# A four-layer graph network on one core: edge scores turned onto feature partitions, and five kept row blocks in the attention layer

## The chip, the cores and the metric

The kernel runs on one core of one Trainium2 chip. The metric is the device time of one execution in microseconds; less is better. Before the change three runs took 4965.81, 4971.25 and 4976.65 us, the median is 4971.25 us.

The engines are named as the profile names them: PE is the matrix engine (PEld its weight loads), DVE the vector engine, ACT the scalar engine, POOL the engine that issues gathers and scatters, SP the one that issues plain DMAs. SBUF is the working memory, PSUM the memory that matmuls write.

## The reference

There are 6250 nodes with 256 features, and 100,000 edges src -> dst, sorted by dst. Four layers follow each other, each ending in a layer norm of x plus the layer's output: a linear layer summed over edges, a two-matrix network on gathered sums, another with weighted edges and batch norms, and an attention layer. What the change touches is the attention layer's score of an edge and its sum:

```
h = lrelu(x @ w_W + w_b)                              # slope 0.2
edge_h = lrelu(edge_attr @ ew_W + ew_b)               # 100000 x 128 by 128 x 256
e = concat(h[src], h[dst], edge_h) @ a_W + a_b        # a_W is 768 x 1
alpha = exp(e - max over the edges of src)  /  their sum over the edges of src
out = sum over the edges of src of alpha * h[dst]
```

The third part of e, edge_h @ a_W[512:768], depends on the inputs only. This "edge score" is computed at the kernel's start, and used at its end.

## The kernel before, in words

The work starts with `prepare` (from L1909). Edges are split into 782 columns of up to 128 edges. Each edge becomes a record of four numbers (target node, place of its source in its block, edge weight, edge score), and the records have to be sorted by source block. For that DVE and PE count edges per block and rank them (`Slots`), and each column's 128 records are scattered to a table in DRAM by one indirect DMA on POOL (`Scatter.columns`, L929). The first 192 columns ("own", PLACED) are not scattered: they are put in place by matmuls with one-hot matrices (`Placed`: `build` makes the matrices on DVE, L880 to L897; `use` multiplies, L909).

The edge scores (`Scores`, L749 to L850) go through the columns in chunks of twelve (STEP), loaded by one DMA each (L802), and in units of four columns. The order of chunks is written out: seven scattered chunks, then sixteen groups of one own chunk and two scattered ones (nine units), then the scattered rest, twelve chunks of which two have one column. There are some 197 units. `turn` transposes a unit's four columns on PE (L813), and ACT copies them out (L815). `score` then makes, for each column, a PSUM tile with the edges on partitions and the 256 features along it: a matmul of three bf16 rows with ones brings the bias (L824), a matmul adds the column's features times the weight in fp32 (L825). A 257th column of the weight holds the part of the score that is linear. DVE reads the tile, takes the maximum with 0, multiplies by 0.8 a and sums (L827), and ACT adds the 257th column and writes the record's score (L829). Then the column may be scattered.

`run` (L833) puts other work between the units: unit i is turned, unit i - 1 scored, an own unit built after two and used after three, and a table of extras adds the second part of the ranks in units 2 to 18 (L728 to L731), the transposes and the first linear layer of 49 node blocks from unit 33 on, three units apart (L357, L364, L1997, L940, L941), and counts of edges by target block from unit 41 on (49 times L2031). This order is a wish: outside of stretches marked manual_schedule the framework's scheduler orders the instructions of each engine itself, as long as data and buffers allow it. Inside such stretches (the attention layer is one) they stand as written. A pool's buffers are handed out in turn, so the next user of a buffer waits for the last one.

When the last record is scattered, `read_lists` (L1677) reads the table back, and the other layers run. The attention layer is `direct_l3` (L1475). It goes through 49 source blocks of 128 nodes; each has 17 tiles of 128 edges (S_TILES), sorted by target block. Tiles whose targets all lie below block H3 are "near": their rows are kept in SBUF (`hot`) and reached by matrices; every other tile's rows are gathered by an indirect DMA (L979). `near_tiles` (L1048) counts the near ones: three of 17 for nearly all blocks. The stages of several blocks are interleaved by a table of steps (L1659):

- `rows` (lag 0) gathers the far tiles; `scores` (lag 1) adds the gathered half of the score (L1539) and spreads scores over partitions by transposes (L1550), four tiles to one PSUM tile.
- `matrices` (lag 2) makes, for each kept block, a matrix from one-hots (L1621: three bf16 parts for each pair of near tile and block), ACT copies it (L1624).
- `largest` takes the maximum (L1560), and asks for the transposes of tiles 12 to 16 after its first step; `parts` and `weights` make the exponents (L1569 to L1603); ACT makes three scaled one-hots for a near tile (L1601) and one for a far tile (L1603).
- `sums` (lag 2) adds far rows (L1630) and kept rows (L1633), fp32, two passes each; `means` and `finish` (lag 3) end the block.
- `masks` (L1514 to L1518) and `near_scores` (L1529, L1532: the kept half of the score for near tiles) prepare the next block on DVE.

Of the kernel before, what the change touches and what calls it, by code (L numbers as in the profile page):

```python
# [7 lines left out]
FT = mybir.dt.float32  # L8
I32 = mybir.dt.int32
AF = mybir.ActivationFunctionType  # L10
OP = mybir.AluOpType
# [39 lines left out]
S_TILES = sum(n for _, _, _, n in STRETCHES)  # L51
TS = NB * S_TILES
S_ROWS = -(-(S_TILES * P * NB + E) // P)
H0, H1, H2, H3 = 24, 16, 9, 3
SURE = 3.5


# [691 lines left out]
class Scores:  # L749
# [4 lines left out]

    STEP = 12

    def __init__(self, k, pool, psum, attr, ew_w, ew_b, a_w, out, ready):
        self.k, self.pool, self.psum, self.attr, self.out, self.ready = k, pool, psum, attr, out, ready
        nc, v = k.nc, k.nc.vector
        self.w = pool.tile([P, D + 1], FT, name="ew_w")  # L760
        nc.sync.dma_start(self.w[:, :D], ew_w)
        self.a = bcast_row(k, pool, a_w[2 * D:3 * D, :], D, "a3")
        self.b = pool.tile([3, D + 1], BF16, name="ew_b8")
        with k.tc.tile_pool(name="score_in", bufs=1) as tmp:
            b = tmp.tile([P, D + 1], FT, name="ew_b")
            nc.sync.dma_start(b[:, :D], bass.AP(tensor=ew_b.tensor, offset=ew_b.offset, ap=[[0, P], [1, D]]))
            for t in (self.w, b):
                scr = tmp.tile([P, D], FT, name="a_scr")
                v.scalar_tensor_tensor(scr, t[:, :D], SLOPE, self.a, op0=OP.mult, op1=OP.mult,
                                       accum_out=t[:, D:D + 1])  # L770
            v.tensor_scalar(self.a, self.a, 1.0 - SLOPE, None, op0=OP.mult)

            here = tmp.tile([3, 3], FT, name="ew_here")
            v.tensor_scalar(here, k.iota_row[:3, :3], k.iota_p[:3, :], None, op0=OP.is_equal)
            part = tmp.tile([3, D + 1], BF16, name="ew_part")
            v.memset(self.b, 0.0)
            for i in range(3):
                v.tensor_copy(part, b[:3, :])
                if i < 2:
                    v.tensor_sub(b[:3, :], b[:3, :], part)  # L780
                v.scalar_tensor_tensor(self.b, part, here[:, i:i + 1], self.b, op0=OP.mult, op1=OP.add)
        self.ones = pool.tile([3, P], BF16, name="ones3")
        nc.gpsimd.memset(self.ones, 1.0)

        own, other = list(range(0, PLACED, self.STEP)), list(range(PLACED, EC, self.STEP)) + [EC]
        self.order = other[:7]
        for i, c in enumerate(other[7:]):
            if i % 2 == 0:
                self.order += own[i // 2:i // 2 + 1]
            self.order.append(c)  # L790
        assert len(self.order) == len(own) + len(other)
        self.units = [(c, min(4, EC - c), P) for c0 in self.order if c0 < EC
                      for c in range(c0, min(c0 + self.STEP, EC), 4)] + [(EC, 1, ET)]
        self.at, self.a_t = {}, {}

    def load(self, c):
        if c % self.STEP and c != EC or c > EC or c in self.at:
            return
        at = self.at[c] = self.pool.tile([P, self.STEP, DE], FT, name="at", bufs=2)
        if c < EC:  # L800
            n = min(self.STEP, EC - c)
            self.k.nc.sync.dma_start(at[:, :n, :],  # L802
                                     self.attr[c * P:(c + n) * P, :].rearrange("(c p) d -> p c d", p=P))
        else:
            self.k.nc.sync.dma_start(at[:ET, 0, :], self.attr[P * EC:E, :])

    def turn(self, pool, i):
        c0, n, n_e = self.units[i]
        at, off = (self.at[EC], 0) if c0 == EC else (self.at[c0 // self.STEP * self.STEP], c0 % self.STEP)
        w_all = (n - 1) * P + n_e  # L810
        pa = self.psum.tile([P, 4 * P], FT, name="ps_a")
        for j in range(n):
            self.k.nc.tensor.transpose(pa[:, j * P:j * P + n_e], at[:n_e, off + j, :], self.k.ident[:n_e, :n_e])  # L813
        a_t = self.a_t[i] = pool.tile([P, 4 * P], FT, name="a_t", bufs=3)
        self.k.nc.scalar.copy(a_t[:, :w_all], pa[:, :w_all])  # L815

    def score(self, pool, i):
        nc = self.k.nc
        c0, n, n_e = self.units[i]
        a_t = self.a_t.pop(i)  # L820
        s = pool.tile([P, 4], FT, name="half", bufs=4)
        for j in range(n):
            z = self.psum.tile([P, D + 1], FT, name="ps_b", bufs=3)
            nc.tensor.matmul(z[:n_e, :], self.ones[:, :n_e], self.b, start=True, stop=False)  # L824
            nc.tensor.matmul(z[:n_e, :], a_t[:, j * P:j * P + n_e], self.w, start=False, stop=True)  # L825
            scr = pool.tile([P, D], BF16, name="scr", bufs=2)
            nc.vector.scalar_tensor_tensor(scr[:n_e, :], z[:n_e, :D], 0.0, self.a[:n_e, :], op0=OP.max, op1=OP.mult,  # L827
                                           accum_out=s[:n_e, j:j + 1])
            nc.scalar.activation(self.out[:n_e, c0 + j:c0 + j + 1], z[:n_e, D:], AF.Identity, bias=s[:n_e, j:j + 1])  # L829
        if c0 >= PLACED:  # L830
            self.ready(c0, c0 + n)

    def run(self, pool, extra):  # L833

        n = len(self.units)
        for i in range(n + 3):
            if i < n:
                c0 = self.units[i][0]
                if c0 in self.order:
                    for c in self.order[self.order.index(c0):][:2]:  # L840
                        self.load(c)
                self.turn(pool, i)
            if 0 <= i - 1 < n:
                self.score(pool, i - 1)
            for lag, f in ((2, "build"), (3, "use")):
                if 0 <= i - lag < n and self.units[i - lag][0] < PLACED:
                    getattr(self.placed, f)(self.units[i - lag][0])
            for f in extra.get(i, ()):
                f()
        assert not any(i > n + 2 for i in extra)  # L850


class Placed:
# [29 lines left out]
    def build(self, c0):  # L883
# [8 lines left out]
        slot = []  # L892
        for j in range(4):
            lo, hi = IN[c0 + j]
            slot.append(self.pool.tile([P, max(h - l for l, h in IN) * P], F32R, name="placed_l", bufs=8))
            nc.vector.tensor_scalar(slot[-1][:, :(hi - lo) * P], k.iota16[:, :(hi - lo) * P],
                                    self.at[:, c0 + j:c0 + j + 1], None, op0=OP.is_equal)  # L897
        self.rhs[c0] = rhs, slot
# [1010 lines left out]
def prepare(k, a, table0, first, rec, placed, ends, idx_d, loc_d, bad):  # L1909
# [6 lines left out]
    with (  # L1916
# [44 lines left out]
        with tc.tile_pool(name="score", bufs=1) as pool:  # L1961
# [29 lines left out]
                transposed(k, x_ts[b], load_block(k, pool, a["x"], b))  # L1991

            def row(b):
                ph = ps.tile([P, D + 1], FT, name="ps_b", bufs=3)[:, :D]
                times(k, ph, x_ts.pop(b), w_t)
                h = pool.tile([P, D], FT, name="h", bufs=2)
                nc.vector.tensor_add(h, bias, ph)  # L1997
# [85 lines left out]
            at(40, blocks)  # L2083
            for b in range(NB):
                at(41 + b // 2, count, b)
            scores.placed = None
            scores.run(pool, extra)


# [50 lines left out]
```

## Time and profile before

| | |
|---|---|
| median of the runs | 4971.25 us |
| the profiled execution | 4276.06 us |
| its span | 4274.2 us |
| mean granted PE clock | 0.925 |
| PE busy | 3609.2 us (84%) |
| DVE busy | 2950.7 us (69%) |
| POOL busy | 2738.1 us (64%) |
| ACT busy | 1476.9 us (35%) |
| L825 with 1564 passes on PE | 548.5 us |
| L929, 590 scatters on POOL | 578.7 us |
| L979 on x, 541, and on rows, 1032 gathers | 557.5 and 1154.2 us |

The profiled execution is one run, and was shorter than the three timed ones. Its page has no row that says why. Busy time is the time in which an engine works on an instruction; for PE the ends are modelled, so that the distance between starts says more than durations. A wait line reads: who waited, for whom, us in total, times, longest. "Issue" is time in which the profile shows nothing that was waited for.

The stages by time: the scores with their scatter 70 to 986 us, layer one to about 1580, layer two to about 2330, layer three to about 3240, the attention layer to the end.

### The profile page before, as it was taken

The numbers are of one execution on the slowest core, as the hardware profiler recorded it, in microseconds if no ns is written. First come the engines' busy times: TensorE is split into PE (matmuls) and PEld (weight loads), VectorE is DVE, ScalarE is ACT, GpSimd is POOL, SyncE is SP. The second block draws the span as 40 slices with busy tenths as digits, with TensorE's granted clock in tenths as the row PEclk, the third lists the DMA queues.
The fourth block names the chain that finished last, engine by engine and source line by source line (L and its number), as shares of the span: only waits on it lengthen the run. The fifth ranks groups of instructions, "written<-read, shape, count | busy, mean of one in ns | idle before, by whom it ended". The sixth has DMA issues, their size and how long they took to land. (4 is left out here: it accounts for less than half of the span.)

```text
span 4274.2 us, 70822 instructions
## 1 busy us (share of the span) xinstructions
PE 3609.2 (84%) x23988; PEld 2791.3 (65%) x23988; DVE 2950.7 (69%) x9234; ACT 1476.9 (35%) x3780; POOL 2738.1 (64%) x2685
## 2 busy tenths in 40 slices
PE   7999999985999988888886999999853777777776
PEld 4566666644999977766665777777532565656565
DVE  7887665544777757878787665565286777777775
ACT  1344334332333322222222111111343455555554
POOL 3765656576777757566663777777303777777774
PEclk9999999997999989989998999999997888888888
DMA  4233333325766775455563333333244444444443
GB/s 82 61 89 91 92 87 84 88 54 140 217 215 210 218 229 166 135 167 173 169 186 92 110 108 107 108 109 108 58 113 126 124 134 142 134 140 136 137 137 91
DMA packets 373432, 552.44 MB, mean 129 GB/s; under 512 B 88710, under 2 KB 265064, under 8 KB 372774
## 3 DMA queue, kind: packets, MB, share of 16 engines
q0 software_dynamic: 136064, 353.87, 29.2%
q1 hardware_dynamic: 236998, 193.96, 15.2%
q8 instruction: 193, 3.16, 0.3%
q14 instruction: 177, 1.45, 0.1%
HBM read 486.32 MB, written 62.09 MB: 128 GB/s over the span
## 5 line engine op out<-in xcount | busy, mean ns | idle before, releaser
L979 POOL DMA_INDIRECT g<-rows,idx_s x1032 | 1154.2, 1118 | 388.2 <-issue 239.0
L929 POOL DMA_INDIRECT rec<-r_s,addr x590 | 578.7, 981 | 337.5 <-ACT r_s L829 227.1
L979 POOL DMA_INDIRECT g<-x,idx_s x541 | 557.5, 1030 | 220.7 <-issue 77.1
L979 POOL DMA_INDIRECT g<-rows,idx_d x383 | 434.7, 1135 | 269.5 <-PE ps_g L986 157.4
L825 PE MATMUL ps_b<-ew_w,a_t 128*128 128x257 f32 x1564 | 548.5, 433 | 2.0 <-ACT a_t L815 2.0
L827 DVE SCALAR_TENSOR_TENSOR scr<-ps_b,a 128x256 bf16<-128x256 f32 x782 | 325.1, 423 | 254.3 <-PE ps_b L825 229.8
L1630 PE MATMUL ps_g<-g,s 128*128 128x257 f32 x1374 | 406.3, 466 | 0.0
L1130 PEld LDWEIGHTS <-od 128*128 128x128 bf16 x5947 | 348.7, 98 | 53.4 <-issue 20.4
L1630 PEld LDWEIGHTS ps_g<-g,s 128*128 128x128 f32 x1374 | 324.2, 240 | 63.5
L1138 PE MATMUL ps_g<-g,cs 128*128 128x256 f32 x1082 | 290.1, 395 | 44.7 <-DMA g<-x,idx_s 43.3
L829 ACT ACTIVATE r_s<-ps_b,half 128x1 f32<-128x1 f32 x782 | 201.1, 263 | 360.5 <-DVE scr L827 355.3
L974 DVE TENSOR_TENSOR os<-iota_row,loc_s 128x768 bf16<-128x768 f32 (+3 forms) x294 | 271.2, 922 | 72.9 <-PE ps_q L1284 62.2
L1092 DVE TENSOR_SCALAR od<-iota,rel 128x128 bf16<-128x128 f16 (+9 forms) x780 | 248.8, 399 | 100.6 <-PE ps_q L1130 96.4
L825 PEld LDWEIGHTS ps_b<-ew_w,a_t 128*128 128x128 f32 x1564 | 233.5, 188 | 97.1 <-ACT a_t L815 2.3
L1133 ACT CAST a_hi<-ps_q 128x512 fp32r<-128x512 f32 x294 | 172.6, 587 | 328.9 <-PE ps_q L1130 321.9
L1550 PE MATMUL ps_a<-ident,ep 128*128 128x128 f32 x833 | 154.8, 315 | 148.5 <-DVE ep L1539 100.1
L1133 ACT COPY a_hi<-ps_q 128x512 f32<-128x512 f32 x146 | 70.0, 480 | 590.2 <-PE ps_q L1130 570.5
L985 PE MATMUL ps_g<-g,cs 128*128 128x256 f32 x728 | 234.1, 338 | 43.0 <-DMA g<-rows,idx_d 41.9
L1138 PEld LDWEIGHTS ps_g<-g,cs 128*128 128x128 f32 x1082 | 186.3, 190 | 106.5 <-DMA g<-x,idx_s 85.4
L1287 ACT CAST a_hi<-ps_q 128x512 fp32r<-128x512 f32 x196 | 114.9, 586 | 381.8 <-PE ps_q L1284 368.3
L985 PE MATMUL ps_g<-first_rows,a_hi 128*128 128x256 f32 x980 | 245.6, 283 | 0.0
L986 PE MATMUL ps_g<-first_rows,a_hi 128*128 128x256 f32 x980 | 244.4, 282 | 0.0
(294 smaller groups left out, 8195.1 us busy)
## 6 DMA issues: line engine op xcount, KB each, us to landing
at<-in_edge_attr SPq DMA_DIRECT2D x65, 768.0 KB
edge_row<-node_row SPq DMA_DIRECT2D x49, 544.0 KB
xb<-x SPq DMA_DIRECT2D x144, 128.0 KB
g<-rows,idx_s POOLq DMA_INDIRECT x1032
xb<-in_x SPq DMA_DIRECT2D x96, 128.0 KB
x<-x SPq DMA_DIRECT2D x96, 128.0 KB
rows<-hl SPq DMA_DIRECT2D x47, 256.0 KB
rec<-r_s,addr POOLq DMA_INDIRECT x590
```

The source lines that it names most:

```text
L825: nc.tensor.matmul(z[:n_e, :], a_t[:, j * P:j * P + n_e], self.w, start=False, stop=True)
L827: nc.vector.scalar_tensor_tensor(scr[:n_e, :], z[:n_e, :D], 0.0, self.a[:n_e, :], op0=OP.max, op1=OP.mult, accum_out=s[:n_e, j:j + 1])
L929: s = nc.gpsimd.indirect_dma_start(out=self.table, out_offset=bass.IndirectOffsetOnAxis(ap=self.addr[:n, c:c + 1], axis=0), in_=self.rec[: ...
L974: k.nc.vector.tensor_tensor(dst, k.iota_row.unsqueeze(1).to_broadcast([P, n, P]), loc.unsqueeze(2).to_broadcast([P, n, P]), op=op)
L979: k.nc.gpsimd.indirect_dma_start(out=dst, out_offset=None, in_=table, in_offset=bass.IndirectOffsetOnAxis(ap=idx, axis=0))
L985: k.nc.tensor.matmul(out, lhs, row[:, :D].bitcast(F32R), start=start, stop=False)
L986: k.nc.tensor.matmul(out, lhs, row[:, D:2 * D].bitcast(F32R), start=False, stop=stop)
L1092: nc.vector.tensor_scalar(od[:, o:o + (hi - lo) * P], k.iota16[:, :(hi - lo) * P], rel[:, s + t:s + t + 1], None, op0=OP.is_equal)
L1130: nc.tensor.matmul(pa[:, j * P:(j + 1) * P], od[:, o:o + P], x[:, t, :], start=(m == 0), stop=(m == len(steps) - 1))
L1133: nc.scalar.copy(a[:, :n, :].rearrange("p j s -> p (j s)"), pa[:, :n * P])
L1138: nc.tensor.matmul(ps, a, row, start=start, stop=stop)
L1630: nc.tensor.matmul(ps, s[:, j, :], g[:, j, :D + 1], start=(j == 0), stop=False)
```

## The change

In the scores the features go onto partitions, and the edges of a unit, 512, along the tile. With a the score's weight and W, b those of the edge features, each output feature's column of W is scaled by |a| (so the product with the edge is |a| p). As |a| lrelu(p + b) = 0.2 |a| b + max(|a| p + 0.8 |a| b, 0.2 |a| p), ACT adds the shift 0.8 |a| b while it copies the product out of PSUM, and DVE takes the maximum of that and of 0.2 times the product, which it reads from PSUM too. The two feature halves are joined by one DVE instruction with the product of their signs, and a matmul with the sign vector, one for each column of edges, sums over partitions. Twelve columns' sums stand in one PSUM tile, to which ACT adds the constant 0.2 a b and writes the records; only then are the twelve scattered, or built and used if they are own. The bias matmuls, the 257th column, and the accumulating DVE instructions go. The PSUM tiles called ps_b become two of 512 columns instead of three of 257 (the node blocks' linear layer uses them too), ps_t is new; a_t has two buffers instead of three, the own columns' one-hots (placed_l) six instead of eight. `sums` runs two units after `hidden`.

In the attention layer H3 goes from three to five. Then four of 17 tiles are near (three in the last block, with 14 gathers left), 13 are gathered; the pairs of near tile and kept block go from six to ten, and the matrices of five blocks take two PSUM tiles instead of one.

```diff
-H0, H1, H2, H3 = 24, 16, 9, 3
+H0, H1, H2, H3 = 24, 16, 9, 5
...
-    def score(self, pool, i):
+    def hidden(self, pool, i):
+        nc = self.k.nc
+        w = self.units[i][1] * P
+        a_t = self.a_t.pop(i)
+        y = pool.tile([P, DK, 4 * P], FT, name="y", bufs=2)
+        for o in range(DK):
+            pz = self.psum.tile([P, 4 * P], FT, name="ps_b", bufs=2)
+            nc.tensor.matmul(pz[:, :w], self.w[:, 0, o * P:(o + 1) * P], a_t[:, :w], start=True, stop=True)
+            z = pool.tile([P, 4 * P], FT, name="z", bufs=3)
+            nc.scalar.activation(z[:, :w], pz[:, :w], AF.Identity, bias=self.shift[:, o:o + 1])
+            nc.vector.scalar_tensor_tensor(y[:, o, :w], pz[:, :w], SLOPE, z[:, :w], op0=OP.mult, op1=OP.max)
+        v = self.v[i] = pool.tile([P, 4 * P], FT, name="v", bufs=3)
+        nc.vector.scalar_tensor_tensor(v[:, :w], y[:, 0, :w], self.signs, y[:, 1, :w], op0=OP.mult, op1=OP.add)
+
+    def sums(self, pool, i):
         nc = self.k.nc
         c0, n, n_e = self.units[i]
-        a_t = self.a_t.pop(i)
-        s = pool.tile([P, 4], FT, name="half", bufs=4)
+        first = self.of(c0)
+        if c0 == first:
+            self.rows[first] = self.psum.tile([P, self.STEP], FT, name="ps_t", bufs=1)
+        pt, v = self.rows[first], self.v.pop(i)
         for j in range(n):
-            z = self.psum.tile([P, D + 1], FT, name="ps_b", bufs=3)
-            nc.tensor.matmul(z[:n_e, :], self.ones[:, :n_e], self.b, start=True, stop=False)
-            nc.tensor.matmul(z[:n_e, :], a_t[:, j * P:j * P + n_e], self.w, start=False, stop=True)
-            scr = pool.tile([P, D], BF16, name="scr", bufs=2)
-            nc.vector.scalar_tensor_tensor(scr[:n_e, :], z[:n_e, :D], 0.0, self.a[:n_e, :], op0=OP.max, op1=OP.mult,
-                                           accum_out=s[:n_e, j:j + 1])
-            nc.scalar.activation(self.out[:n_e, c0 + j:c0 + j + 1], z[:n_e, D:], AF.Identity, bias=s[:n_e, j:j + 1])
-        if c0 >= PLACED:
-            self.ready(c0, c0 + n)
+            c = c0 - first + j
+            nc.tensor.matmul(pt[:, c:c + 1], v[:, j * P:(j + 1) * P], self.sign[:, 1:2], start=True, stop=True)
+        end = c0 + n
+        if end - first == self.STEP or end == EC or c0 == EC:
+            nc.scalar.activation(self.out[:n_e, first:end], pt[:n_e, :end - first], AF.Identity, bias=self.same[:n_e, :])
+            self.ready(first, end)
...
             if 0 <= i - 1 < n:
-                self.score(pool, i - 1)
-            for lag, f in ((2, "build"), (3, "use")):
-                if 0 <= i - lag < n and self.units[i - lag][0] < PLACED:
-                    getattr(self.placed, f)(self.units[i - lag][0])
+                self.hidden(pool, i - 1)
+            if 0 <= i - 3 < n:
+                self.sums(pool, i - 3)
+            if self.todo:
+                for f, c in self.todo.pop(0):
+                    f(c)
...
+    def ready(self, c0, c1):
+        if c0 >= PLACED:
+            self.scatter(c0, c1)
+        else:
+            p, c = self.placed, range(c0, c1, 4)
+            for i in range(len(c) + 1):
+                self.todo.append([(p.use, x) for x in c[max(i - 1, 0):i]] + [(p.build, x) for x in c[i:i + 1]])
...
-            slot.append(self.pool.tile([P, max(h - l for l, h in IN) * P], F32R, name="placed_l", bufs=8))
+            slot.append(self.pool.tile([P, max(h - l for l, h in IN) * P], F32R, name="placed_l", bufs=6))
...
-                ph = ps.tile([P, D + 1], FT, name="ps_b", bufs=3)[:, :D]
+                ph = ps.tile([P, D], FT, name="ps_b", bufs=2)
```

In the steps ahead, "L837" is the new matmul with the sign vector, "L821" the new product, by their lines in the changed file; all other lines are those of the kernel before.

## The prediction

> **What bounds the kernel now.** I read the engines' busy time by 100 us first, to find the stages that the change touches: the scores with their scatter (70 to 986 us), and the attention layer (from 3271 us). Columns: stretch, busy us and instructions of PE, PEld, DVE, ACT, POOL, then granted clock, DMA share, GB/s.
> ```profile
> 300.00:400.00 100.00, 99.83 (x461) 61.44 (x461) 85.28 (x342) 40.11 (x129) 59.42 (x61) 1.00 0.32 87
> 700.00:800.00 100.00, 100.00 (x466) 61.43 (x463) 63.75 (x235) 38.90 (x131) 52.62 (x53) 1.00 0.31 86
> 800.00:900.00 100.00, 100.00 (x440) 58.00 (x439) 48.20 (x208) 41.69 (x135) 74.07 (x77) 1.00 0.32 87
> 900.00:1000.00 100.00, 47.83 (x199) 25.24 (x198) 31.51 (x124) 19.41 (x65) 72.88 (x73) 0.76 0.19 53
> 3800.00:3900.00 100.00, 71.22 (x446) 58.45 (x444) 74.19 (x242) 58.13 (x155) 78.06 (x73) 0.88 0.46 136
> ```
> In the scores PE is full until 946 us at full clock; DVE has 15 to 36% free; POOL waits, then fills up at the end. Whether PE is really full, its timeline says, since its ends are modelled:
> ```profile
> 603.23 0.60 PE L813 MATMUL ps_a<-ident,at 128*128 128x128 f32 x4
> 603.76 0.28 PE L824 MATMUL ps_b<-ew_b,ones 3*128 3x257 bf16 x1
> 603.97 0.70 PE L825 MATMUL ps_b<-ew_w,a_t 128*128 128x257 f32 x2
> 604.61 0.28 PE L824 MATMUL ps_b<-ew_b,ones 3*128 3x257 bf16 x1
> ```
> Starts lie 0.84 us apart per column without a hole: a unit of four columns takes 4 x 0.843 + 4 x 0.109 (transposes) = 3.81 us, the distance from one unit's L813 to the next (603.23 to 607.04). So PE sets the pace. Then the waits of 150 to 900 us and of the attention layer (3285 to 4225 us):
> ```profile
> POOL rec L929 <- ACT r_s L829: 211.1, 183, 11.3
> DVE scr L827 <- PE ps_b L825: 205.7, 391, 2.2
> ...
> POOL g L979 <- issue: 183.4, 602, 0.3
> DVE ep L1539 <- DMA g<-rows,idx_s: 88.1, 46, 7.8
> DVE w L1593 <- ACT ce L1589: 63.3, 48, 1.4
> DVE far L1560 <- PE ps_a L1550: 46.6, 74, 2.0
> ```
> POOL waits for scores once per group of nine units (one own chunk that isn't scattered, two others that are): its restarts are at 186.4 us, then every 41 us or so, the sixteenth at 801; from there it runs 185 us unbroken to 986, 40 us behind PE. In the attention layer POOL waits for nothing (0.3 us of issue before each gather), while DVE waits 88.1/48 = 1.84 us a block for gathers: POOL sets the pace there, DVE is just behind.
>
> **The change part by part: scores.** Per unit PE loses four L824 and four L825 pairs (4 x 0.843 = 3.37 us). It gains two matmuls 128x512 in fp32, two passes each; L370 has that shape, its passes start 0.429 us apart: 4 x 0.429 = 1.72. It gains four L837, with a fresh fp32 stationary v and one column. No row has this. Its pass must load 128 fp32 columns: the transposes L813, which do that too, start 0.109 us apart, so 4 x 2 x 0.109 = 0.87. The Trainium skill would allow both less and this: "TensorE: Matmul & The Clock Gate", Back-to-back issue gap, gives up to 64 columns 60 cycles (25 ns), hence 0.2 us a unit; its LDWEIGHTS section gives columns/1.2 ns, 107 ns a load. L1579 (bf16, 3 columns) does start 25 ns apart, L813 in fp32 does not; I take the loads. From above, if the load isn't hidden at all (0.188 us, the L825 row), 1.5 us. New unit: 0.44 + 1.72 + 0.87 + 0.12 for changes of operand = 3.15 us, saving 0.66 (0.03 to 1.3).
> A group took 41.3 us by this: 9 x 3.81, three node blocks (L357, L364: 1.1 each) and three L909 sets (1.25 each). After: 9 x 3.15 + 7.05 = 35.4.
>
> DVE: four L827 are 0.345 us apart with their accumulator reads, 1.38 a unit. After: two STT 128x512 from PSUM and one from SBUF. L827 lasts 0.423 for 256 elements, so 0.69 for 512 (256 more at 0.96 per ns); independent ones start 0.07 earlier, the last has to await its input: 0.62 + 0.73 + 0.62 = 1.97. So +0.59 a unit, +5.3 a group. Late groups are busy 0.63 x 41 = 25.8 us, after that 31.1: fits in 35.4. Early groups (to about 400 us) also hold 49 counts of 1.08 us: 0.853 x 41 = 35.0, after that 40.3: DVE takes over and nothing is won there. The first seven chunks don't count; POOL sets them.
>
> ACT: four r_s of 0.263 become two of 0.684 (L1330's row) and a twelfth-column one per three units: 1.64 to 2.0 us a unit, hidden under 3.15; if not, it is only latency for the two ps_b tiles. These fall from three of 257 columns to two of 512, shared with the node rows: a tile is held 0.86 + 0.2 + 0.68 + 0.69 = 2.4 us, so PE runs ahead by less than one unit, and a build (1.38 + 4 x 0.35 us on DVE, its slots down from eight to six, so that it also awaits L909) stalls it. I put 2.6 us a group for that (0 to 8): 38 us. What queues behind a DVE that awaits L909 are the y of the next unit, and behind these PE.
>
> Scatters are released per 12 columns, by a matmul two units later, so about four units x 3.9 = 16 us later. The first 25 units, with the ranks on DVE, take 5.0 us each and DVE is busy 79% of that (100 to 200 us): 3.95 + 0.59 = 4.54, some stalls: I take 0.35 us won on each, 9 back. The first restart moves from 186 to 193. The placed records' builds and uses move two to four units back with it; they issue no DMA, and the at loads keep their order on SP's queue. Then four early groups at 40 (before 39): 353; eleven late ones at 38 (before 41.7): 771, against 801. POOL's last 185 us remain: 956, plus contention. A rule speaks against the change here: "SBUF — State Buffer", Who interferes with whom, says that a DVE instruction with two SBUF inputs contends with a GpSimd one that reads SBUF. L827 had one such input, the new sum v has two. The trace agrees with the rule:
> ```profile
> 3659.77 2.42 DVE L1518 TENSOR_TENSOR own<-iota,loc 128x2176 bf16<-128x2176 f16 x1
> 3660.28 2.73 POOL L979 DMA_INDIRECT g<-rows,idx_s  x1 [0.30 <-issue]
> ```
> That gather takes 2.73 us instead of 0.95. By the rule taken to its full, v costs 0.62 per unit, 19 us over the last 30 units; by L1647 (0.42 us beside a gather of 1.16), 0.2. I take 0.1 to 0.15 a unit, as only half the v meet a scatter's start: 4 us. The scores end at 960: **26 us won** (-30 to 60). Setup instructions change by some 1 us; free if hidden by the loads.
>
> **Attention layer.** The tiles wholly below block 5 are four of 17 instead of three. POOL: one of 14 gathers of 1.25 us goes. A block took 19.72 us (own to own: 3279.7 to 4226.2, 48 steps): 14 x 1.25 + 2.2 of contention; after: 18.45, + 0.3 by the new two-input op = 18.75. DVE: one more L1529/L1532 pair at 512 wide; 384 wide takes 0.89 us, 128 more 0.18: +1.07. PE: matrices 6 to 10 pairs x 3, +12 L1621 at 0.056 warm or 0.107 cold (+0.67, +1.28); this stands ahead of the last transposes that L1560 awaits: with slack 0.36 warm and none cold, a third of the time cold, +0.6 on DVE's chain. Two hot rows more, one far less: +0.43, hidden under the chain from L1573 to L1539; if cold, up to 0.9. ACT: three osw for one s, +0.6 of 11 in 19. So DVE's round is 19.72 - 1.84 + 1.07 + 0.6 = 19.55 and takes over from POOL: 48 x 0.17 = **8 us won** (-40 to 47, the ends being cold throughout, and POOL's 18.75). H3's two more rows are loaded once, 1 to 2 us.
>
> Sum: 26 + 8 - 1 = 33. The profiled execution takes 4276.1 us (span 4274.2 and 2 around it), hence 4243. The median of the runs shown is 4971.3, 695 more, of which the page shows nothing; I carry 33 over unscaled, 4938. In proportion it would be 38.
>
> **Rivals.** (1) The floors are reached: no stalls, late groups at 35.4 (26 + 11 x 2.6 = 55 won), attention at 18.75 (48 x 0.97 = 47): 102 us, or 118 in proportion to the median: 4853 to 4869. For it: PE 100% and POOL never waiting; against it: DVE at 88% of such a group. (2) Slower: the two ps_b tiles couple PE to DVE. Each of 48 builds holds DVE for up to 3.6 us in one piece, PE has 0.9 us of slack (3.15 less the 2.4 hold, rounded up for queueing) and loses 2.7: 8 us a group against the 5.9 won, and the late start of 16 us remains: 16 x 2.1 + 7 = 41 slower, 5012. It decides from 2 us lost per build. Against it: in the built order the builds are interleaved with y and v. (3) No change: DVE sets every group, the late scatters eat the rest, the attention layer swaps POOL for DVE: 4971.
>
> **Numbers.** Likeliest 0.43, 4938; floors 0.20; coupling 0.22; no change 0.15. A measurement of this kernel can tell 0.2% (10 us) from none. Faster 0.62, same 0.14, slower 0.24. Range 4860 to 5005: from between the floors' two ends to most of the coupling's price. Likeliest alone: 4905 to 4965.
>
> **What would show it.** L821 passes 0.43 apart and L837 0.109: if 0.19, the PE saving is gone. POOL's restarts every 38 us after 400, 40 before; last scatter near 960. PE waiting for DVE's y on ps_b over 100 us in all means coupling. In the attention layer DVE's wait for gathers falls from 88 towards 0 and POOL begins to wait; own to own 19.5. Wrong if POOL still never waits at 18.75, or if the transposes hold L1560 over 2 us a block.

## The result, and the profile after

The changed kernel takes 5237.07 us (median of 4 runs, 5215.12 to 5268.15), beside 4968.53 us for the kernel before (4 runs): ratio 1.0543, 95% interval 1.0507 to 1.0578, slower by 269 us where 33 us less were forecast. The profiled execution took 5215.12 us (span 5213.3), with a mean granted PE clock of 0.838.

One thing has to be known to read any number below: whole series of runs of this kernel go at one of two paces, about 4280 us or 4960 to 5050 us for the kernel before, and the profile shown ahead of the prediction was of the first while the times shown were of the second. I call them the short and the long pace; ratios are always taken within one series.

The stretches shown of before, now of the changed kernel (same columns: PE, PEld, DVE, ACT, POOL, then clock, DMA share, GB/s):
```profile
300.00:400.00 100.00, 80.11 (x337) 50.63 (x336) 75.35 (x151) 37.63 (x76) 47.47 (x48) 0.86 0.26 72
700.00:800.00 100.00, 78.00 (x348) 52.22 (x347) 53.87 (x100) 35.73 (x71) 46.88 (x47) 0.80 0.22 62
800.00:900.00 100.00, 79.34 (x356) 54.88 (x356) 52.29 (x99) 35.79 (x71) 33.93 (x35) 0.77 0.21 60
900.00:1000.00 100.00, 81.96 (x373) 57.38 (x373) 56.98 (x105) 37.77 (x76) 46.17 (x47) 0.83 0.26 72
3800.00:3900.00 100.00, 41.62 (x272) 34.78 (x273) 43.22 (x139) 31.99 (x91) 52.94 (x53) 0.65 0.33 87
```
Nothing is full: PE has gaps in the scores, every engine is idle for nearly half the time or more in the attention layer, and the granted clock is lower (0.77 to 0.86 in the first three rows, where it was 1.00, and 0.65 in the last, where it was 0.88). The last scatter comes at 1262 us (before: 986), a block of the attention layer takes 29.04 us from own to own (before: 19.72). The waits say for what (the scores, 150 to 900 us, then the attention layer, 3785 to 4900 us):
```profile
POOL rec L949 <- ACT r_s L840: 313.2, 20, 30.8
...
ACT z L823 <- remote: 110.7, 28, 12.2
...
POOL g L999 <- PE ps_g L1650: 445.7, 36, 17.2
ACT mats L1644 <- remote: 380.8, 58, 14.2
DVE far L1580 <- remote: 373.8, 38, 12.6
```
"Remote" means that a semaphore changed just before the start, and that no instruction of the trace ended shortly before that could have changed it. Those waits take some ten microseconds, about once a block, on ACT and DVE at once. One of them in the timeline of the changed kernel (start, duration, engine, line; in brackets the idle time before it):
```profile
4107.97 1.84 PE L1641 MATMUL ps_q<-osw,od 128*128 128x128 bf16 x30
...
4109.65 0.71 PE L1570 MATMUL ps_a<-ident,ep 128*128 128x128 f32 x5
...
4110.41 0.95 POOL L999 DMA_INDIRECT g<-rows,idx_s  x1 [0.30 <-issue]
...
4117.92 0.94 POOL L999 DMA_INDIRECT g<-rows,idx_s  x1 [0.30 <-issue]
4121.19 0.75 ACT L1644 COPY mats<-ps_q 128x512 f32<-128x512 f32 x2 [13.97 <-remote]
4121.31 0.75 DVE L1580 CUSTOM_DVE_ANT_0 far<-ps_a,off,m 128x512 bf16<-128x512 f32 x1 [11.90 <-remote]
```
PE's thirty matmuls and its last five transposes are recorded as done by 4110.4. ACT and DVE, which need nothing else, start at 4121.2, 3.3 us after the last gather of POOL's burst started (a burst is a row of gathers without a pause). The only semaphore that the copy waits for is PE's, so PE's signal was late; I call that a hold. The first profile of before had none, and that can be seen in one row of its page, the shares of the chain that ended last:
```profile
DVE 7%; PE 5%; POOL 5%; DMA 4%; issue 2%; ACT 1%; DVEq 0%; SPq 0%; POOLq 0%
```
The same row of the changed kernel:
```profile
DVE 12%; another core or an unknown queue 10%; PE 2%; issue 2%; ACT 2%; DMA 1%; DVEq 0%; POOL 0%; SPq 0%
```

### The profile page after: what moved, and what is told of

Its sections match the earlier page's. It is cut to its first block, busy times and chain, and to the rows that moved or that the text cites. A ratio compares the mean times of both kernels' runs of the same rounds, so it can differ in the third digit from the quotient of the medians.

```text
span 5213.3 us, 70269 instructions
## 1 busy us (share of the span) xinstructions
PE 3762.1 (72%) x24682; PEld 2965.5 (57%) x24682; DVE 3065.6 (59%) x8403; ACT 1584.8 (30%) x3606; POOL 2623.0 (50%) x2635
## 5 line engine op out<-in xcount | busy, mean ns | idle before, releaser
L999 POOL DMA_INDIRECT g<-rows,idx_s x983 | 1045.5, 1064 | 946.8 <-PE ps_g L1650 554.8
L821 PE MATMUL ps_b<-a_t,ew_w 128*128 128x512 f32 (+1 forms) x788 | 478.1, 709 | 144.1 <-DVE y L824 50.0
L824 DVE SCALAR_TENSOR_TENSOR y<-ps_b,z 128x512 f32<-128x512 f32 (+1 forms) x394 | 266.8, 683 | 328.8 <-ACT z L823 271.8
L1580 DVE CUSTOM_DVE_ANT_0 far<-ps_a,off,m 128x512 bf16<-128x512 f32 x196 | 127.6, 651 | 529.7 <-remote 483.1
L823 ACT ACTIVATE z<-ps_b,shift 128x512 f32<-128x512 f32 (+1 forms) x394 | 268.6, 684 | 543.6 <-PE ps_b L821 286.8
L1599 PEld LDWEIGHTS <-eq 128*128 128x128 bf16 x833 | 29.6, 104 | 583.5 <-issue 583.4
L837 PEld LDWEIGHTS ps_t<-sign,v 128*128 128x128 f32 x1564 | 232.5, 220 | 129.8 <-issue 58.3
L1150 PE MATMUL ps_q<-osw,od 128*128 128x128 bf16 x3063 | 228.1, 224 | 96.7 <-issue 77.0
L821 PEld LDWEIGHTS ps_b<-a_t,ew_w 128*128 128x128 f32 x788 | 150.6, 224 | 228.0 <-DVE y L824 77.5
L1153 ACT CAST a_hi<-ps_q 128x512 fp32r<-128x512 f32 x294 | 166.8, 586 | 340.3 <-PE ps_g L1006 195.9
```

Source lines behind the costliest of these rows:

```text
L821: nc.tensor.matmul(pz[:, :w], self.w[:, 0, o * P:(o + 1) * P], a_t[:, :w], start=True, stop=True)
L823: nc.scalar.activation(z[:, :w], pz[:, :w], AF.Identity, bias=self.shift[:, o:o + 1])
L824: nc.vector.scalar_tensor_tensor(y[:, o, :w], pz[:, :w], SLOPE, z[:, :w], op0=OP.mult, op1=OP.max)
L999: k.nc.gpsimd.indirect_dma_start(out=dst, out_offset=None, in_=table, in_offset=bass.IndirectOffsetOnAxis(ap=idx, axis=0))
L1150: nc.tensor.matmul(pa[:, j * P:(j + 1) * P], od[:, o:o + P], x[:, t, :], start=(m == 0), stop=(m == len(steps) - 1))
L1153: nc.scalar.copy(a[:, :n, :].rearrange("p j s -> p (j s)"), pa[:, :n * P])
```

## The experiments

"Own to own" below is the mean distance of L1518 (L1538 in the changed file) over 48 steps, the length of a block in the attention layer.

**1. Is the first profile an ordinary execution, and which part loses?** Three kernels in one series: before unchanged; before with `H3 = 5`; the new scores with `H3 = 3`.
```diff
-H0, H1, H2, H3 = 24, 16, 9, 3
+H0, H1, H2, H3 = 24, 16, 9, 5
```


> The kernel before, unchanged, for a second profile. The profiled execution shown of it was 695 us shorter than the timed ones, and the changed kernel's profiled execution is not shorter than its timed ones (5215 us to 5237). Theory: both kernels have stretches in which PE's signals reach ACT and DVE late, while POOL's gathers or scatters go on, and the first profile of before happened to have none. Then this profile lies near 4970 us, with the missing 700 us in stalls of all three compute engines: in the scores, layer one to three and the attention layer. Rival: profiling itself makes this kernel quick; then the profile is again near 4275 us and the timed ones near 4970.

> The kernel before with H3 = 5, scores as before. If the attention layer costs what its step in the prediction left out (theory: the longer block of matmuls ahead of the transposes is where late signals fall, 26 us a block instead of 20): slower by 100 to 250 us, 5070 to 5220. If the attention layer is as predicted (DVE takes over from POOL): 4955 to 5000. If the loss lies in the scores alone: 4960 to 4970.

> The changed kernel with H3 = 3. If the scores lose by the coupling of PE and DVE over the two ps_b tiles, or by late signals: slower by 50 to 250 us, 5020 to 5220. If the scores are as predicted: about 4940. Together with the run of H3 = 5 alone the two differences should add up to about 268 us if the parts don't act on each other.

Measured, beside 5040.38 us: before again 5041.19 (ratio 1.0001, 0.9979 to 1.0023), five blocks alone 5275.5 (1.0457, 1.0410 to 1.0503), the scores alone 5077.35 (1.0067, 1.0036 to 1.0099). One of the twelve executions of before took 13073.43 us and is left out of the ratio; no trace of it is kept, and why it took so long isn't known. The profiled execution of before took 5041.15 us here, so it isn't the profiling that made the first one short. It has holds as well; its waits from 3785 to 4900 us:
```profile
POOL g L979 <- PE ps_g L1630: 295.6, 42, 27.6
DVE far L1560 <- remote: 214.6, 51, 10.1
ACT mats L1624 <- remote: 201.0, 31, 11.9
```
With five blocks alone the same waits are twice as long:
```profile
DVE far L1560 <- remote: 432.1, 35, 14.3
ACT mats L1624 <- remote: 429.3, 63, 15.0
```
A block takes 25.68 us in before, 30.75 with five blocks alone, 26.10 with the new scores alone. So the kernel before already loses 6 us a block and some 250 us in the scores (last scatter at 1244) against its first profile (the layers between lose 230 us more), and nearly all of the change's loss, 48 x 5.1 = 243 us, is the five row blocks'.

**2. Do the gathers make the holds?** The attention layer gathers for its first four blocks (and the last) only, and then uses those rows again, so that its sums are of other rows:
```diff
-        g = made[b, "g"] = pool.tile([P, nf, W3], FT, name="g3", bufs=4)
+        if b < 4:
+            kept[b] = pool.tile([P, nf, W3], FT, name=f"g3_{b}", bufs=1)
+        g = made[b, "g"] = kept[b % 4]
+        if b >= 4 and near[b] == near[b % 4]:
+            return
```


> The kernel before, its attention layer gathering rows for its first four blocks (and the last) alone; the later blocks use those rows again, so the layer's sums are of other rows. Theory (PE's signals arrive late while POOL gathers, and that is what makes a block long in ordinary executions): without gathers the waits ended by nothing that the trace shows (far and mats, 5.2 us a block each in the run of before) go, and with them POOL's pace; a block falls from 25.7 to 18 to 19.5 us, the busy time of DVE and its chain to the weights; whole time about 5041 - 47 x 6.7 = 4725, ratio 0.93 to 0.945. Rival (the cold clock and the chain from DVE through PE to ACT make the block long, the gathers stand beside it): a block stays above 23 us, ratio over 0.97.

> The same with five row blocks kept (before's scores), and no gathers after the first four blocks. Theory: the 5.1 us a block that five row blocks cost is time in which PE's signals are held; without gathers it goes, and a block takes 0 to 1.5 us more than with three row blocks and no gathers (DVE's own work, about +1 us): 19 to 21 us, ratio 0.935 to 0.96. Rival (the twelve more matmuls of the matrices and the second copy out of PSUM lengthen the chain itself): it stays 4 to 5 us a block, 200 us, above the kernel with three row blocks and no gathers.

Measured, beside 4957.79 us: three blocks 4653.85 (0.9381, 0.9325 to 0.9436), five blocks 4748.67 (0.9572, 0.9522 to 0.9622). A block takes 18.43 and 20.27 us. Of the waits of three blocks without gathers that are ended by "remote", 3950 to 4800 us, this is left:
```profile
DVE far L1564 <- remote: 3.2, 1, 3.2
DVE ce L1590 <- remote: 2.9, 1, 2.9
```
The holds come with the gathers: without them five blocks cost 1.84 us a block, with them 5.1. The 1.84 is a little above the 1.5 I had put as the most.

**3. What in five blocks lengthens the holds?** The order of two steps, and the number of matmuls (one bf16 part in place of three), each with five blocks and before's scores:
```diff
-    steps = ((rows, 0), (scores, 1), (matrices, 2), (largest, 1), (parts, 1), (sums, 2),
+    steps = ((rows, 0), (scores, 1), (largest, 1), (parts, 1), (matrices, 2), (sums, 2),
```
```diff
-                steps = [(t, i) for t in range(near[b]) if w[t][0] <= d < w[t][1] for i in range(3)]
+                steps = [(t, i) for t in range(near[b]) if w[t][0] <= d < w[t][1] for i in range(1)]
```


> Five row blocks (before's scores), the matrices' matmuls and copies put behind the two steps that find the largest score and its parts, in place of ahead of them; the same work. Rival (the matrices' matmuls stand ahead of what DVE waits for, so every one of the twelve more costs its time): a block loses 4 to 5 us against five row blocks in the old order, 30.7 to 26, ratio to before about 1.0. Theory (the burst of gathers after each release of their buffer sets the hold, whatever is queued then): within 2 us a block of the old order, ratio 1.03 to 1.06.

> Five row blocks (before's scores), the matrices made of the first of the three bf16 parts of the weights alone: 10 matmuls a block in place of 30, so the weights lose their lower bits. Rival (PE's added matmuls): 20 x 0.22 = 4.4 us of PE a block go, a block falls from 30.7 to 26.3, ratio about 1.005. Theory (holds of the signals): PE's matmuls are recorded as done long before the hold ends, so taking them out ends nothing earlier; within 1.5 us a block, ratio 1.03 to 1.05.

Measured, in the series of 2: other order 5087.95 (1.0246, 1.0201 to 1.0291), a block 27.08 us; one part 4920.47 (0.9914, 0.9870 to 0.9959), a block 23.48 us. My theory fell in the form in which I had written it: fewer matmuls do shorten the block, by 7.3 us, more than their time on PE (20 x 0.056 to 0.107 = 1.1 to 2.1 us), and the order, with the work unchanged, takes back 3.7 us. The waits of the kernel with one part, 3950 to 4800 us, have hardly a hold, though POOL gathers as before:
```profile
DVE far L1560 <- remote: 40.6, 17, 6.5
...
ACT mats L1624 <- remote: 17.7, 5, 5.2
```
So I measured over all blocks after 3900 us how long after the recorded end of the matrices' last matmul the last copy starts, and how far into POOL's burst that end falls (medians, us):

| kernel | matmuls | end falls into the burst at | copy starts later by |
|---|---|---|---|
| five blocks, one part | 10 | 8.9 | 0.6 |
| before again | 18 | 8.3 | 2.8 |
| five blocks alone | 30 | 6.3 | 10.9 |
| the changed kernel | 30 | 6.5 | 8.0 |
| five blocks, other order | 30 | 16.2 (21 blocks), a burst lasting some 17 | 2.6 |
| five blocks, no gathers | 30 | no burst | 0.4 |

(A second copy behind the first one starts after 0.4 us when nothing is held, a single copy after 0.04.) The kernels with fewer matmuls also end them later in the burst, so place and number have to be told apart. In the blocks whose matmuls end within the first 6.6 us of a burst, the copy is late by 2.7 us after ten (8 blocks), by 3 to 5 us after eighteen (medians of three traces) and by 8 to 13 us after thirty (four traces), here mostly to the burst's end, 10 us on. So the number counts at the same place, though not in proportion; and later in a burst the same number costs less. The theory that was left when I wrote the next expectations: what PE does in the first part of a burst has its signals held (or is done later than recorded, as PE's ends are modelled); outside of a burst it costs what it seems to.

**4. The matmuls ahead of the burst.** The weights and matrices of the next block are put ahead of the last far matmul, so that they end before the buffer comes free; the work is the same:
```diff
         for j in range(n - near[b]):
+            if j == n - near[b] - 1 and b + 1 < NB:
+                weights(b + 1)
+                matrices(b + 1)
             nc.tensor.matmul(ps, s[:, j, :], g[:, j, :D + 1], start=(j == 0), stop=False)
...
+    def first(b):
+        if b == 0:
+            weights(b)
+            matrices(b)
+
+    steps = ((rows, 0), (scores, 1), (largest, 1), (parts, 1), (sums, 2), (first, 1), (means, 3),
```
Beside it, the kernel before with two thirds of its eighteen matmuls done again (`steps += steps[:2 * len(steps) // 3]`), and two kernels whose scatters are left out after the first call.

> Five row blocks (before's scores), with the weights and the matrices' thirty matmuls of the next block put ahead of the last far matmul of a block's sums, so that they are through before that matmul frees the gather buffer and POOL begins its burst; the same work. Theory as the last runs left it (what PE does in the first part of a burst of gathers has its signals held, up to the burst's end; thirty matmuls fall there, ten do not): the copies out of PSUM no longer wait for a hold, a block falls from 30.7 to 22 to 24.5 us, ratio to before 0.96 to 0.985. Rival (thirty matmuls cost their time on PE wherever they stand): a block stays above 27 us, ratio over 1.01.

> The kernel before (three row blocks, one copy out of PSUM, fourteen gathers) with its eighteen matmuls of the matrices raised to thirty by doing two thirds of them again into the same sums, so the near rows' weights are partly counted twice. If the number of matmuls in the burst brings the hold: a block goes from 25.7 to 29 to 31 us, ratio 1.03 to 1.05, nearly all of the change's cost. If the second copy and its PSUM tile, or the thirteen gathers, bring it: 12 x 0.1 = 1.2 us a block at most, ratio 1.00 to 1.015.

> The kernel before with all its scatters of records left out but the first call's, so that the later layers work on empty records; the scores alone are looked at. Theory (POOL's indirect transfers hold PE's signals in the scores too): the last unit's turn comes near 950 us in place of 1240, the pace of the first profiled execution, with PE busy without a gap. Rival (the transfers have no part in it): it stays above 1150.

> The new scores with three row blocks, the scatters left out in the same way. My prediction's account of PE (3.81 us a unit before, 3.15 after, and placing unchanged) gives its last unit 25 to 45 us ahead of the kernel before without scatters, near 910 to 925 us; if the coupling through the two PSUM tiles counts where nothing is held either, it is level or behind.

This series ran at the short pace: before took 4278.9 us, on the chip on which it had taken 4957.79 us in the series of 2 and 3. So it couldn't test the holds. It gave: five blocks with the matmuls early 4214.87 (0.9846, 0.9825 to 0.9866), a block 18.39 us; three blocks with thirty matmuls 4261.85 (0.9967, 0.9949 to 0.9986), a block 19.48 us, so at this pace twelve more matmuls cost the block nothing: their signal came within 0.1 us. DVE waits longer for the transposes behind them (86.6 us from 3285 to 4225 us where before waited 46.6), and less for gathers (48.3 where it was 88.1), as POOL sets the pace there. The test of their number alone at the long pace is missing. Without scatters the copy of the last unit (L815, L812) came at 947.0 us in before's scores (946.4 in the first profile, with scatters) and at 823.9 us in the new ones: 123 us earlier, where I had expected 25 to 45. At the short pace the scatters cost PE nothing, so this says nothing of the long one. (The two executions took 13.2 and 13.3 ms: with records missing, the kernel's count of misplaced edges (`bad`) isn't zero, and a second, general path behind the direct one (`general`, L1803) does all four layers again. It was about as long as the one odd execution of step 1.)

**5. The change and its parts again.** The changed kernel, the new scores alone, five blocks alone, and the changed kernel with the edit of 4.

> The changed kernel, unchanged. The kernel before has now been seen at two paces, 4960 to 5040 us in some series and 4279 us in another (its first profile, 4276 us, too). If the loss of 5 per cent belongs to the slow pace: beside a kernel before of about 4280 us the change gains what its own profile allows, 33 us by my sum and up to 160 us where the scores' stage without scatters points, ratio 0.96 to 0.995; beside one of about 5000 us it loses again, 1.05. If the loss belongs to the change itself: 1.03 to 1.06 beside either.

> The new scores alone (three row blocks). Beside a kernel before of about 4280 us: last unit between 835 us (without scatters it was 824) and 920 us (my sum), ratio 0.97 to 0.993. Beside one of about 5000 us: 1.00 to 1.01 as before.

> Five row blocks alone (before's scores). Beside a kernel before of about 4280 us: a block from 19.7 to 18.4 to 19.7 us (the reordered kernel took 18.4), ratio 0.985 to 1.00. Beside one of about 5000 us: 1.045 as before.

> The changed kernel with the weights and the matrices' matmuls of the next block ahead of the last far matmul of a block's sums, so that they are through before the burst of gathers. Beside a kernel before of about 5000 us: if the holds that the burst brings are what five row blocks cost, a block falls from 29 or 30.7 to 22 to 24.5 us and the ratio from 1.054 to 0.96 to 1.00; if the matmuls cost their time wherever they stand, it stays above 1.03. Beside one of about 4280 us: within 10 us of the changed kernel.

The series ran at the long pace, 4973.56 us. The changed kernel took 5250.42 us (1.0575, 1.0483 to 1.0667; 29.39 us a block), the new scores alone 4998.78 (1.0051, 1.0031 to 1.0070; 24.90 us), five blocks alone 5232.05 (30.58 us; its four executions lie between 5116 and 5248 us, too far apart for a ratio), and the changed kernel with the matmuls early 5020.47 (1.0110, 1.0038 to 1.0182; 24.87 us a block). Four fifths of the loss go with work that was only moved, though the block and the ratio lie a little above the 22 to 24.5 us and the 0.96 to 1.00 that I had expected. The holds at the copies are gone; a shorter one has appeared at the sums of the weights (3950 to 4800 us of that kernel):
```profile
DVE ce L1606 <- remote: 244.7, 33, 9.0
...
DVE far L1580 <- remote: 2.2, 2, 1.2
```

**6. The change at the short pace.** The changed kernel once more, and the kernel of 4.

> The changed kernel once more, for the pace of the kernel before that this series has. Beside about 4280 us: ratio 0.96 to 0.995 if the loss belongs to the slow pace, 1.03 or more if it belongs to the change. Beside about 5000 us: 1.05 to 1.06, as twice before.

> Before's scores, five row blocks, and the thirty matmuls ahead of the last far matmul (0.985 beside a kernel before of 4279 us). Beside about 5000 us: a block of 24 to 25 us as in the changed kernel so reordered, against before's 25.7, and no loss in the scores: ratio 0.98 to 1.00, and 0.935 to 0.95 against five row blocks in the old order. Beside about 4280 us: 0.985 again.

This series ran at the short pace, on the chip of 2 to 4: before 4275.01 us. The changed kernel took 4242.12 us: ratio 0.9926 (0.9910 to 0.9943), 32.9 us less. Five blocks with the matmuls early took 4208.46 (0.9844, 0.9827 to 0.9860), the best full computation of the study at this pace.

**7. Three blocks, matmuls early.**

> The kernel before (three row blocks) with its eighteen matmuls of the matrices ahead of the last far matmul too; the same work. Beside a kernel before of about 5000 us: its own waits ended by nothing that the trace shows at the copies (4.9 us a block) go; as DVE waits for the weights' chain instead (the reordered changed kernel showed 7.4 us a block there), a block falls from 25.7 to 24 to 25 us, ratio 0.985 to 1.00. Beside about 4280 us: POOL's 14 gathers (18.45 to 18.75 us) set the pace, a block from 19.7 to 18.8 to 19.5, ratio 0.988 to 0.998, behind the 0.984 of five row blocks so ordered.

At the long pace (5052.17 us): 5059.58, ratio 1.0005 (0.9983 to 1.0027), 25.93 us a block. No gain: the hold only moves to the sums of the weights (279.9 us in 32 waits, 3950 to 4800 us, no longer any at the copies). So the edit takes away what five blocks add, and not the 6 us that a block of the kernel before has over the short pace. No kernel that does the whole computation beat before at the long pace.

## Why the prediction was wrong, point by point

**The step that failed** is "I carry 33 over unscaled". The sum was made on an execution of 4276 us and handed to a median of 4971, with the remark that the page shows nothing of the 695 us between. At the pace of that profile the change gave 33 us (32.9 measured); at the pace of the times it cost 269. The term that went wrong most is the five row blocks': 0.17 us a block won by the sum, 5.1 us lost as measured at the long pace (30.75 against 25.68 us), 243 of the 269 us. The scores, 26 us won by the sum, lost 25 and 37 us in two series.

The 695 us were not a surcharge to be passed over. In the profile of step 1 (765 us longer than the first) 258 of them lie in the scores, 286 in the attention layer and 229 in the layers between; the short rest behind the last block is 7 us shorter. In the attention layer the holds are at work, and the sums of PE's and DVE's work stop deciding there. In the scores holds are not what fills the time: in before, only 23 us of the waits between 150 and 900 us are ended by "remote". What differs there is the granted clock (first profile, then step 1):
```profile
150.00:900.00 750.00, 749.81 (x3403) 451.67 (x3402) 513.73 (x1982) 299.42 (x987) 454.34 (x461) 1.00 0.32 87
150.00:900.00 750.00, 696.17 (x2594) 400.90 (x2593) 418.17 (x1594) 224.45 (x747) 339.17 (x346) 0.81 0.24 66
```
PE is busy for 93% of the time, but does 2594 matmuls where it did 3403. By an estimate of mine, 696 x 0.81 = 564 us of PE at full clock stand against 750: 54 us of the 186 missing are gaps of PE, the rest is the clock. Whether gaps lower the clock, or something else does, isn't shown.

Another trace of the pace needs care. The records of the moments at which the eight semaphores of POOL's transfers change number 40,428 for 2546 transfers in the first profile, 15.9 each, so that 16 or 40,736 seem due, but 14,075 in the same kernel at the long pace (in the changed kernel 39,792 and 12,977 of 39,952). That doesn't show signals arriving in bunches, since records are missing too. The packets of 4 bytes, 16 a transfer, end at 39,688 distinct moments in the first profile and at 39,670 at the long pace, as spread out as before, and the large packets took nearly as long (226 and 233 ns on the mean). And of some 1600 DVE instructions that wait for DVE's own semaphore and start 35 ns after the instruction before them, 441 have no record of that update at the long pace, and 2 at the short one: the signal was in time and its record isn't there. What puts a series at the long pace isn't shown by anything here (nor whether the recording of the trace takes part); one chip had both within the hour.

**The scores** were forecast at 26 us and gave 74 at the short pace (last scatter 986.1 to 912.1), beyond the range given. The stretches of that execution:
```profile
300.00:400.00 100.00, 91.69 (x476) 61.33 (x476) 91.90 (x249) 50.28 (x103) 72.67 (x68) 1.00 0.35 89
700.00:800.00 100.00, 99.77 (x544) 69.89 (x543) 72.80 (x119) 60.91 (x117) 75.59 (x75) 1.00 0.36 99
800.00:900.00 100.00, 29.55 (x154) 19.69 (x152) 21.68 (x36) 18.84 (x37) 76.52 (x78) 0.65 0.10 24
```
PE's account held: L821 passes 0.429 us apart, L837 0.111 (0.109 forecast; eight in 0.95 us below), late groups of nine units 34 to 36 us (35.4). So did the durations on DVE: y takes 0.68 us (0.69 summed) and v 0.74 (0.73). The 0.96 elements per ns used there are those of L1560 in before: 512 columns take 0.75 us, 128 take 0.35. (ACT's 1.64 us a unit comes out only if the records are written once a unit; once in three gives 1.46. Nothing hung on it.)
```profile
639.71 1.02 PE L821 MATMUL ps_b<-a_t,ew_w 128*128 128x512 f32 x2
...
640.58 0.95 PE L837 MATMUL ps_t<-sign,v 128*128 128x1 f32 x8
```
Two terms were mis-sized. The 2.6 us a group for the two ps_b tiles weren't paid; the waits of the changed kernel at this pace, 150 to 900 us:
```profile
POOL rec L949 <- issue: 154.2, 505, 0.5
...
POOL rec L949 <- ACT r_s L840: 31.3, 11, 6.8
PEld ps_b L821 <- DVE y L824: 30.0, 60, 2.6
...
PE ps_b L821 <- DVE y L824: 8.3, 15, 1.8
```
The weight loads do wait for y, but the matmuls only 8.3 us in all, 0.4 of it after 400 us. And the early groups, where I had DVE take over at 40.3 us, took 30 to 38 (two of them 45). PE ends at 831 us in place of 948, and what comes next is POOL: with so little waiting it runs from 84 to 912 us, 590 scatters of 1.40 us each. My picture of a release per group and 185 us after the last one no longer fits; no release bounds the stage. As POOL now binds, the contention that the Trainium skill describes ("SBUF — State Buffer", Who interferes with whom), which I put at 4 us, costs more: the 127 scatters that start while a sum v runs last 1.211 us on the mean, the other 463 1.009, so 127 x 0.202 = 26 us. All 590 last 1.052 us against 0.981 before, 42 us more; the other 16 us aren't explained. At the long pace all this is worth less than nothing (+25 and +37 us in the two series): PE's work is shorter, but PE is busy some 80 us of 100 where before's was busy 93, both at a mean clock of 0.81, and waits ended by "remote" come to 121 us on ACT and 55 on DVE between 150 and 900 us. I made no experiment that takes the loss of the scores apart at that pace.

**The attention layer** was forecast to win 8 us and lost 38 at the short pace (19.72 to 20.50 us a block; 19.55 forecast). DVE took over from POOL as forecast: its wait for gathers fell from 88.1 to 16.1 us and POOL has begun to wait. The waits from 3215 to 4190 us of that execution:
```profile
DVE far L1580 <- PE ps_a L1570: 119.8, 96, 2.7
...
POOL g L999 <- PE ps_g L1650: 76.2, 38, 2.4
```
The mis-sized term is the wait of L1560 for the transposes behind the matrices' matmuls. I put 0.6 us on DVE's chain; the wait went from about 1 us a block (46.6 us in 48 blocks) to 2.5, beyond the 2 us named as the point at which I'd be wrong. The twelve matmuls alone account for 0.8 of the 1.5 us: in three blocks with thirty matmuls (step 4) the wait is 86.6 us. What brings the other 0.7 isn't shown. Moving the weights and all thirty matmuls, as in step 4, takes the wait away (9.2 us in all), and a block takes 18.4 us, below the floor of 18.75 of my first rival.

At the long pace the added matmuls, at the same place, lengthen the holds: 5 us a block. Shown: the gathers are needed (without them 1.8 us a block, and a signal within 0.4 us); with five blocks, ten matmuls in place of thirty take the loss away; and moved out of the burst the thirty cost a block nothing (24.87 us, against 24.90 for three row blocks in the same series). That the place in the burst counts too, the table of step 3 shows. Thirty matmuls that merely run late at their usual pace wouldn't look like a hold: in 13 of the 43 holds at the copies in step 5's changed kernel the four updates of PE's semaphore that were due are all on record, within 0.14 us, while the recorded ends of the four lie some 0.7 us apart; and the transposes behind the thirty start 0.06 us after the start of the last of them. So PE's updates come late and together. What keeps them back is open, and so is what gathers do to them, as the packets are hardly slower. The test of the number alone, with three row blocks, fell in a series at the short pace; the kernel with one part differs from five blocks by the number alone, which is why it speaks.

**The rivals.** None was the right one. "Slower" was given 0.24, nearly all of it for a coupling through ps_b that cost next to nothing at the short pace and wasn't tested at the long one; that the kernel did get slower had another cause. The sum's agreement at the short pace, 33 for 33, is luck: two errors that cancel (74 for 26, -38 for +8, and 3 us lost elsewhere).

## What to carry to other kernels

If the profiled execution's time is 16% off the times shown, the stages that account for it come first; a change must not be summed on a profile of another pace and carried over. In this kernel a chain with a share for "another core or an unknown queue" on one core (1 to 11% at the long pace, none at the short one), and waits ended by "remote", went with late signals: a chain of thirty matmuls that others await cost 5 us a block more inside a burst of gathers, and next to nothing ahead of the event that starts the burst. Missing records of semaphores alone say nothing of the signals. When a stage's limit is lifted, redo the whole sum for the next engine, its contention included; and read the busy time of PE together with the clock.

## What the hardware did that I hadn't expected

In whole series of runs, and not in others, PE's signals arrive late while POOL issues indirect transfers without a pause: 8 to 13 us after the recorded end of thirty bf16 matmuls (medians of four traces), 2.7 us after ten at the same place in the burst, and within 0.4 us without gathers or at the short pace, with the packets hardly slower. The late updates come together, within 0.14 us where four are on record.
